# Half of the skip product moved one block earlier, input transposes put between its sums, and the norm's root moved to GpSimd, in the attention layer of a two-layer kernel

## The chip, the cores and the metric

The kernel runs on one core of a Trainium2 chip. The metric is the device time of one execution in microseconds (us); smaller is better. A core has five engines that each work through their own list of instructions in order: PE (TensorE, matrix products and transposes), ACT (ScalarE), DVE (VectorE), POOL (GpSimd) and SP (SyncE, which here issues nearly all DMA transfers). An instruction that needs another engine's result waits for a semaphore, and everything behind it on its own engine waits with it. That holds for SP too: a DMA whose source is not ready yet holds up the DMAs listed behind it.

## The reference

Two layers, each added to its input. The first one is an attention over 8 batches of 1024 tokens with 512 channels and 16 heads of 32; it is the one that the change touches. Cut to what matters:

```python
x = x * s1[:, None, :]                       # s1, s2: halves of cond
mu = jnp.mean(x, axis=-1, keepdims=True)
var = jnp.mean(jnp.square(x - mu), axis=-1, keepdims=True)
x = (x - mu) * jax.lax.rsqrt(var + EPS_IN)
q = heads(jnp.einsum('bsh,oh->bso', x, q_weight) * q_dc[:, None, :])
k = heads(jnp.einsum('bsh,oh->bso', x, k_weight) * k_dc[:, None, :])
v_flat = jnp.einsum('bsh,oh->bso', x, v_weight) * v_dc[:, None, :] * s2[:, None, :]
skip = v_flat
v = heads(v_flat)
attn = jax.nn.softmax(jnp.einsum('bhqd,bhkd->bhqk', q, k) * scale, axis=-1)
out = jnp.einsum('bhqk,bhkd->bhqd', attn, v).transpose(0, 2, 1, 3).reshape(B, S, H)
out = jnp.einsum('bsh,oh->bso', out, w_weight) * w_dc[:, None, :]
skip = jnp.einsum('bsh,oh->bso', skip, u_weight) * u_dc[:, None, :]
return out + skip
```

The second layer (a gated state-space scan over 1024 steps) follows and is not touched.

## The kernel before, in words

**Blocks and slots.** The attention is a hand-written pipeline. A batch b has four blocks o = 0 to 3; a block is four heads. A block has 16 slots: 8 query tiles of 128, times two pairs of heads. Slot n issues, in this order: in odd n only, the product of an earlier slot pair's probabilities with the values (`weigh`, L303, on PE); the scores of two heads (L286 and L289); their maxima on DVE (L447); transposes of the slot before's first head (`flip`, L296) with their copies on ACT (L454); the two exponentials on ACT (L457); some pieces of background work; the transposes of the second head, with their two copies on DVE (L468, L473); more pieces of background work; and the scaling of the probabilities by 1/sum on POOL (L462, L471, L476), which waits for reciprocals on DVE (L461, L470, L475). With `weigh` at the head of the odd slots, the time from one slot's first score product to the next slot's is longer behind an even slot than behind an odd one.

**Background pieces.** `background(n)` is a generator that yields once for each 128x512 product (four of them make one sum of a `chain`, L130) or for each group of four input transposes (`turn`, L111). Its work by block is: o = 0 and 1: the projections of the next block (`project`, 6 sums, 24 pieces), then half of the output product of the batch before (`out_w`, 4 sums, 16 pieces). o = 2: the projections of block 3 (24), then the transposes of the first half of the next batch's inputs (`turn`, 4). o = 3: the transposes of the second half (4), the projections of the next batch's first block (24), then the whole skip product (`out_u`, 8 sums, 32). Behind the projections, each block calls `fetch_w(n + 2)`, which loads the three weight tiles (w_q, w_k, w_v, 256 KB each, two buffers each) that the projections of the next block will use. What is left of a generator at the end of a block is run out before the next block starts.

**How many pieces a slot gets.** A table gives the pieces of a block, and `due` spreads them; `late` of them come behind the second transposes:

```python
PIECES = {0: 40, 1: 40, 2: 28, 3: 60}
few = max(1, (pieces - 2 * NQ + NQ) // SB)        # NQ = 8, SB = 16
due = few * (done - done // 2) + -(-(pieces - NQ * few) * (done // 2) // NQ) - ran
late = (due + 1 - n % 2) // 2
```

So with 28 pieces an even slot gets 1 and an odd one 2 or 3; with 40 it is 2 and 3; with 44 it would be 2 and 3 or 4; with 60 it is 3 and 4 or 5. The last block of all has its own line for `due`.

**Evacuations and buffers.** All sums and turns share one ring of two PSUM buffers (`ps_m`, tag "mm"), so a sum can start when the sum or turn two places before it has been copied out. The projections are copied out by ACT (L208, L212, L217), `out_u` and `out_w` by DVE with the addition of a loaded tile (L251, L267), and then stored by SP (`xu_d`, L252); turns are copied out by ACT for even k and by DVE for odd k (L113, L115). A finished q half is copied by SP to the other half of the partitions by two DMAs (`moved`, L201 and L202), which wait for ACT.

**The order on SP.** It is the order in which the generators reach their `dma_start`. In blocks 0, 1 and 2 the fetch of w_q, w_k, w_v stands behind the `moved` pair of the last q half of that block's projections; in block 3 too, with `out_u`'s loads (xr from xT, w_u) and stores behind it.

**The norm.** `aside(n)` loads the next batch's inputs in block 1 and runs `normalise` for one half in block 1 and for the other in block 2, one piece at the end of each slot: one slot with the loads, four multiplications on POOL (L84), four pairs of statistics on DVE (L88, L89), then in one piece the square root on ACT (L91), its reciprocal on DVE (L92) and one more small DVE operation (L93), and four scalings on POOL (L101). The piece with the root ends slot 9, so it stands just ahead of slot 10. The exponentials and the square root need different ACT tables, and each change between them is an ACT_TABLE_LOAD.

Of the kernel before, what the change touches and what calls it, by code (L numbers as in the profile page):

```python
# [8 lines left out]
F32 = mybir.dt.float32  # L9
BF16 = mybir.dt.bfloat16  # L10
AF = mybir.ActivationFunctionType
ALU = mybir.AluOpType
# [4 lines left out]
P = 128  # L17
B = 8
H = 512
KH = H // P  # L20
# [7 lines left out]
EPS = 1e-5  # L28
# [4 lines left out]
def modulated_attention(ctx, tc, const, xp, tok, x1_d, xu_d, S, x, xT, cond, wT, ident, condT, early, handover):  # L33
# [9 lines left out]
    nc = tc.nc  # L43
# [10 lines left out]
    own = ctx.enter_context(tc.tile_pool(name="own", bufs=1))  # L54
    sT = own.tile([P, 2 * KH, B], F32, name="sT")
    nc.sync.dma_start(out=sT, in_=condT.rearrange("(k p) b -> p k b", p=P))
    eps = own.tile([P, 1], F32, name="eps_h")
    nc.vector.memset(eps, EPS)
    dc = own.tile([P, 5, KH, B], F32, name="dc")
# [3 lines left out]
    def load_x(b, hf):  # L63

        xq = tok.tile([P, 4, H], F32, name="xq")
        src = x[b, hf * HW : (hf + 1) * HW].rearrange("(j p) c -> p j c", p=P)
        if b == 0:
            nc.sync.dma_start(out=xq[:, 0:2], in_=src[:, 0:2])
        else:
            nc.sync.dma_start(out=xq, in_=src)  # L70
        sr = tok.tile([P, H], F32, name="sr")
        nc.sync.dma_start(out=sr, in_=cond[b, 0:H].unsqueeze(0).to_broadcast([P, H]))
        if b == 0:
            nc.sync.dma_start(out=xq[:, 2:4], in_=src[:, 2:4])
        return xq, sr

    def normalise(xs, first=False):


        xq, sr = xs  # L80
        mv = small.tile([P, 4, 2], F32, name="mv")
        rs = small.tile([P, 4, 2], F32, name="rs")
        for j in range(4):
            (nc.vector if first else nc.gpsimd).tensor_mul(xq[:, j], xq[:, j], sr)  # L84
            yield
        for j in range(4):
            stat = small.tile([P, 6], F32, name="stat")
            nc.vector.bn_stats(stat, xq[:, j])  # L88
            nc.vector.bn_aggr(mv[:, j], stat)  # L89
            yield  # L90
        nc.scalar.activation(rs[:, :, 0], mv[:, :, 1], AF.Sqrt, bias=eps)  # L91
        nc.vector.reciprocal(rs[:, :, 0], rs[:, :, 0])  # L92
        nc.vector.scalar_tensor_tensor(  # L93
            rs[:, :, 1], mv[:, :, 0], -1.0, rs[:, :, 0], ALU.mult, ALU.mult
        )
        yield
        for j in range(4):
            if first and j % 2 == 0:
                nc.scalar.activation(xq[:, j], xq[:, j], AF.Identity, bias=rs[:, j, 1:2], scale=rs[:, j, 0:1])
            else:  # L100
                nc.gpsimd.tensor_scalar(xq[:, j], xq[:, j], rs[:, j, 0:1], rs[:, j, 1:2], ALU.mult, ALU.add)  # L101
            yield

    def turn(xs, put):

        xh = xp.tile([P, KH, HW], F32, name="xh")
        put(xh)
        for k in range(KH):
            ps = ps_m.tile([P, 4, P], F32, tag="mm", name="mm_ps")
            for j in range(4):  # L110
                nc.tensor.transpose(ps[:, j], xs[0][:, j, k * P : (k + 1) * P], ident)  # L111
            if k % 2 == 0:
                nc.scalar.copy(xh[:, k], ps.rearrange("p j t -> p (j t)"))  # L113
            else:
                nc.vector.tensor_copy(xh[:, k], ps.rearrange("p j t -> p (j t)"))  # L115
            yield
# [4 lines left out]
    def half(hf):  # L121
        return slice(hf * HW, (hf + 1) * HW)
# [3 lines left out]
    def chain(pieces, evac):  # L126

        ps = ps_m.tile([P, HW], F32, tag="mm", name="mm_ps")
        for k, (w, x) in enumerate(pieces):
            nc.tensor.matmul(ps, w, x, start=(k == 0), stop=(k == KH - 1))  # L130
            if k < KH - 1:
                yield
        evac(ps)
        yield
# [6 lines left out]
    def load_full(name, pool, tag):  # L141
        w = pool.tile([P, KH, H], F32, tag=tag, name="w")
        nc.sync.dma_start(out=w, in_=wT[name].rearrange("(k p) o -> p k o", p=P))
        return w
# [35 lines left out]
    def load_w(name, o, room=None):  # L180
        w = ring.tile([P, KH, P], F32, tag=f"w_{room or name}", name=f"w_{name}")
        nc.sync.dma_start(
            out=w, in_=wT[name][:, o * P : (o + 1) * P].rearrange("(k p) o -> p k o", p=P)
        )
        return w
# [47 lines left out]
    def load_xr(src, o, hf):  # L233
        xr = ring.tile([P, HW], F32, tag="xr", bufs=3, name="xr")
        nc.sync.dma_start(out=xr, in_=src[o * P : (o + 1) * P, half(hf)])
        return xr

    def out_u(b, vTs, w0):

        todo = [(o, hf) for o in range(KH) for hf in range(2)]  # L240
        ws, xrs = {0: w0}, {todo[0]: load_xr(xT[b], *todo[0])}
        for n, (o, hf) in enumerate(todo):
            c = half(hf)
            if n + 1 < len(todo):
                xrs[todo[n + 1]] = load_xr(xT[b], *todo[n + 1])
            if hf == 0 and o + 1 < KH:
                ws[o + 1] = load_w("u", o + 1)
            xr = xrs.pop((o, hf))

            def evac(ps):  # L250
                nc.vector.scalar_tensor_tensor(xr, ps, udc[:, o, b : b + 1], xr, ALU.mult, ALU.add)  # L251
                nc.sync.dma_start(out=xu_d[b % 2, o * P : (o + 1) * P, c], in_=xr)  # L252

            yield from chain([(ws[o][:, k], vTs[k][:, c]) for k in range(KH)], evac)
# [54 lines left out]
    sts = {bo: {} for bo in blocks}  # L309
# [3 lines left out]
    def fetch_w(n):  # L313

        if n < len(blocks):
            wts[n] = {name: load_w(name, blocks[n][1]) for name in "qkv"}
# [3 lines left out]
    first = [load_x(0, 0)]  # L320
# [16 lines left out]
        next(demods["v"])  # L337
    fetch_w(1)

    def background(n):  # L340

        nonlocal xh_now
        b, o = blocks[n]
        if o < 2 and b > 0:
            w0 = load_w("w", 2 * o)
        if o == KH - 1:
            w0 = load_w("u", 0)
        if n == 1:
            tables = early(xp.tile([P, KH * HW], F32, tag="xh", name="tmp"), ps_m)
            next(tables)  # L350
        if n == 0:
            yield from demods["v"]
            yield from project(
                wts[0], xh_now, 0, 0, sts[0, 0], (("v", 0), ("v", 1), ("q", 1))
            )
            rest = [load_full(name, tok, "xq") for name in "wu"]
        if o < KH - 1:
            yield from project(wts[n + 1], xh_now, b, o + 1, sts[b, o + 1])
            if o == 2 and b + 1 < B:
                yield from turn(xs_next[0], xh_next.append)  # L360
        elif b + 1 < B:
            yield from turn(xs_next[1], xh_next.append)
            xh_now = list(xh_next)
            xh_next.clear()
            yield from project(wts[n + 1], xh_now, b + 1, 0, sts[b + 1, 0])
        fetch_w(n + 2)
        if n == 0:
            yield from demod((3, 4), rest)
        if o < 2 and b > 0:
            yield from out_w(  # L370
                b - 1, [sts[b - 1, k]["a"] for k in range(KH)], [(k, hf) for k in (2 * o, 2 * o + 1) for hf in range(2)], {2 * o: w0}
            )
        if o == KH - 1:
            yield from out_u(b, [sts[b, k]["v"] for k in range(KH)], w0)
        if n == 1:
            yield from tables
        if n == len(blocks) - 1:
            ws = {k: load_w("w", k, "wqkv"[k]) for k in range(KH)}
            last_w.append(out_w(
                b, [sts[b, k]["a"] for k in range(KH)], [(o, hf) for hf in range(2) for o in range(KH)], ws  # L380
            ))
            yield
            for _ in range(4 * KH):
                yield next(last_w[0])
# [8 lines left out]
            yield from normalise(xs_next[o - 1])  # L393

    xs_next, xh_next, last_w = [], [], []
    PIECES = {0: 40, 1: 40, 2: 28, 3: 60}
    probs = None
    flipped = {}
    bg, side, ran, ripe = iter(()), iter(()), 0, 0
    for n in range(len(slots) + 2):  # L400
        bo, q, pair = slots[n] if n < len(slots) else (None, None, None)
        if n % SB == 0:
# [4 lines left out]
            bg, side, ran = iter(()), iter(()), 0  # L407
# [4 lines left out]
        due = 0  # L412
        if bo is not None:

            done, pieces = n % SB + 1, (54, 29)[n // SB] if n < 2 * SB else PIECES[bo[1]]
            few = max(1, (pieces - 2 * NQ + NQ) // SB)
            due = few * (done - done // 2) + -(-(pieces - NQ * few) * (done // 2) // NQ) - ran
            if n < 3:
                due = 6
            if n // SB == len(blocks) - 1:  # L420

                due = -(-33 * min(done, 10) // 10) + 16 * max(done - 10, 0) // 6 - ran
            due = max(due, 0)
            ran += due

# [2 lines left out]
        if n % 2 == 1 and m >= 0:  # L428
            mbo, mq, _ = slots[2 * m]
# [715 lines left out]
```

## Time and profile before

| what | value |
|---|---|
| median of 3 runs | 5712.75 us (5705.14 to 5713.35) |
| the profiled execution | 5708.03 us, its span 5706.3 us |
| busy share of the span | PE 97%, DVE 77%, ACT 69%, POOL 27% |
| first score product of the first slot | 52.3 us |
| first score product of the last slot | 3317.0 us |
| blocks 0, 1, 2, 3 of batch 2 | 98.01, 99.12, 92.99, 116.38 us |
| the last batch's blocks 0, 1, 2 | 98.01, 98.01, 91.57 us |
| mean granted TensorE clock | 0.991 |

The times of blocks and slots are differences between the starts of the first L286 of each, from the timeline of PE. The profiled execution stands 4.7 us under the median and 2.9 us over the fastest run. The attention takes some 3300 us of the span and the scan the rest. In the timeline a row is: start in us, duration in us, engine, line, operation, output <- inputs, form, count, and in brackets the idle time of the engine just before it with what ended it. An engine with a "q" behind its name is its instruction queue (SPq issues DMAs). One 128x512 product in f32 makes two matmul records, each about 0.43 us apart.

### The profile page before, as it was taken

The numbers are of one execution on the slowest core, as the hardware profiler recorded it, in microseconds if no ns is written. First come the engines' busy times: TensorE is split into PE (matmuls) and PEld (weight loads), VectorE is DVE, ScalarE is ACT, GpSimd is POOL, SyncE is SP. The second block draws the span as 40 slices with busy tenths as digits, with TensorE's granted clock in tenths as the row PEclk, the third lists the DMA queues.
The fourth block names the chain that finished last, engine by engine and source line by source line (L and its number), as shares of the span: only waits on it lengthen the run. The fifth ranks groups of instructions, "written<-read, shape, count | busy, mean of one in ns | idle before, by whom it ended". The sixth has DMA issues, their size and how long they took to land.

```text
span 5706.3 us, 113668 instructions
## 1 busy us (share of the span) xinstructions
PE 5525.4 (97%) x43312; PEld 3178.8 (56%) x43312; DVE 4382.9 (77%) x6874; ACT 3959.9 (69%) x6995; POOL 1540.4 (27%) x1667
## 2 busy tenths in 40 slices
PE   7999999999999999999999989999999999999998
PEld 4565656656556556656556555555555555555553
DVE  4666666766766766766666659999999999999996
ACT  5565655655655655655655558898988888888886
POOL 2343433433434434434433310111111111111111
PEclk9999999999999999999999989999999999999999
DMA  2102212112112112112021248888888888888886
GB/s 83 35 24 64 53 44 67 31 55 57 31 58 53 38 50 67 24 53 71 18 65 41 71 123 233 236 238 237 238 238 234 237 235 238 235 238 236 238 238 188
DMA packets 377216, 714.85 MB, mean 125 GB/s; under 512 B 198320, under 2 KB 280512, under 8 KB 347488
## 3 DMA queue, kind: packets, MB, share of 16 engines
q1 hardware_dynamic: 346704, 684.81, 44.4%
q0 software_dynamic: 29968, 22.77, 1.5%
q8 instruction: 344, 5.64, 0.4%
q14 instruction: 200, 1.64, 0.1%
HBM read 596.66 MB, written 83.89 MB: 119 GB/s over the span
## 4 chain that ended last, share of the span: by engine, by line
PE 63%; DMA 15%; DVE 9%; ACT 8%; issue 3%; SPq 2%; POOL 0%; DVEq 0%; ACTq 0%; POOLq 0%
PE mm_ps L130 17%; PE t_ps L296 15%; DMA xb<-xd 10%; PE s_ps L286 9%; PE t_ps L303 8%; DVE h L933 4%; PE in_ps L668 4%; PE y_ps L920 3%; ACT xb L911 2%; PE g_ps L823 2%; SPq L901 2%; DMA out<-o_sb 2%; ACT pr L457 2%; PE o_ps L860 1%; DMA xd<-xt 1%
## 5 line engine op out<-in xcount | busy, mean ns | idle before, releaser
L447 DVE TENSOR_REDUCE nmax<-s_ps 128x1 f32<-128x1024 f32 x1024 | 1206.2, 1220 | 460.7 <-PE s_ps L289 459.9
L454 ACT COPY pT<-t_ps 128x512 f32<-128x512 f32 x1024 | 550.3, 589 | 1298.9 <-PE t_ps L296 1298.4
L933 DVE CUSTOM_DVE_ANT_0 h<-h,xb,lim 128x1024 f32<-128x1024 f32 x1024 | 1373.5, 1341 | 90.0 <-ACT xb L911 41.2
L296 PEld LDWEIGHTS t_ps<-ident,pr 128*128 128x128 f32 x8192 | 912.2, 141 | 658.9 <-issue 491.7
L911 ACT ACTIVATE xb<-xb,ws 128x1024 f32<-128x1024 f32 x1024 | 1177.8, 1164 | 60.2 <-DMA xb<-xd 45.0
L457 ACT ACTIVATE pr<-s_ps,nmax 128x1024 f32<-128x1024 f32 x1024 | 1139.5, 1127 | 5.0 <-DVE nmax L447 4.8
L296 PE MATMUL t_ps<-ident,pr 128*128 128x128 f32 x8192 | 1096.9, 277 | 28.4 <-ACT pT L454 24.7
L476 POOL TENSOR_SCALAR pr<-pr,rinv 128x1024 f32<-128x1024 f32 x512 | 572.2, 1118 | 130.0 <-DVE rinv L475 123.0
L286 PE MATMUL s_ps<-kT,qT 32*128 32x512 f32 x2048 | 596.0, 641 | 2.5 <-ACT pr L457 1.7
L289 PE MATMUL s_ps<-k,q 32*128 32x512 f32 x2048 | 578.0, 640 | 1.1 <-DMA q<-qT 1.1
L462 POOL TENSOR_SCALAR pr<-pr,rinv 128x1024 f32<-128x1024 f32 x256 | 286.8, 1121 | 1070.7 <-PE t_ps L296 751.4
L920 PE MATMUL y_ps<-h,yw 128*32 128x512 f32 x4096 | 527.3, 610 | 36.6 <-DVE y_ps L755 31.6
L303 PEld LDWEIGHTS t_ps<-pT,vt 128*32 128x32 f32 x16384 | 433.9, 110 | 207.6 <-DVE rinv L470 112.9
L303 PE MATMUL t_ps<-pT,vt 128*32 128x128 f32 x16384 | 506.9, 274 | 19.1 <-DVE pT L468 12.3
L471 POOL TENSOR_SCALAR pr<-pr,rinv 128x1024 f32<-128x1024 f32 x256 | 286.2, 1118 | 844.6 <-DVE rinv L470 795.7
L668 PE MATMUL in_ps<-x,win 128*128 128x256 f32 x2048 | 492.2, 386 | 3.8 <-ACT xb L892 3.8
L823 PE MATMUL g_ps<-win,x1t 128*128 128x512 f32 x1024 | 470.5, 602 | 4.0 <-ACT x1t L818 3.6
L860 PE MATMUL o_ps<-wout,xt 128*128 128x512 f32 x1024 | 458.5, 595 | 0.0
L872 POOL DMA_DIRECT2D out<-o_sb x256 | 151.0, 595 | 1053.0 <-ACT o_sb L866 953.3
L668 PEld LDWEIGHTS in_ps<-x,win 128*128 128x128 f32 x2048 | 376.9, 193 | 95.2 <-ACT xb L892 26.2
L786 POOL DMA_DIRECT2D bca<-few x256 | 129.1, 515 | 1019.1 <-ACT few L779 1013.5
L468 DVE COPY pT<-t_ps 128x512 f32<-128x512 f32 x512 | 352.0, 687 | 56.1 <-PE t_ps L296 55.6
(157 smaller groups left out, 6975.4 us busy)
## 6 DMA issues: line engine op xcount, KB each, us to landing
xb<-xd SPq DMA_DIRECT2D x1792, 256.0 KB
xd<-xt SPq DMA_DIRECT2D x64, 512.0 KB
q<-qT SPq DMA_DIRECT2D x128, 128.0 KB
xr<-in_xT SPq DMA_DIRECT2D x64, 256.0 KB
xu_d<-xr SPq DMA_DIRECT2D x64, 256.0 KB
xr<-xu_d SPq DMA_DIRECT2D x64, 256.0 KB
x_d<-xr SPq DMA_DIRECT2D x64, 256.0 KB
out<-o_sb POOLq DMA_DIRECT2D x256, 64.0 KB, 6.0
```

What stands on the lines that cost most here:

```text
L130: nc.tensor.matmul(ps, w, x, start=(k == 0), stop=(k == KH - 1))
L286: nc.tensor.matmul(s_ps[i][:, 0:HW], st["q"][r, qc], st["k"][r, 0:HW], start=True, stop=True)
L289: nc.tensor.matmul(s_ps[i][:, HW:S], st["q2"][r, qc], st["k2"][r], start=True, stop=True)
L296: nc.tensor.transpose(ps[:, j], pr[:, c0 : c0 + P], ident)
L303: nc.tensor.matmul(av[r], vt[:, kt, r], pT[:, i, kt], start=(kt == 0), stop=(kt == KT - 1), skip_group_check=True,)
L447: nc.vector.tensor_reduce(nmax[i], s_ps[i], AX.X, ALU.max, negate=True)
L457: nc.scalar.activation(fresh[i], s_ps[i], AF.Exp, bias=nmax[i], accum_out=rsum[i])
L668: nc.tensor.matmul(ps, win[kk][:, k * P : (k + 1) * P], st["x1"][:, kk].rearrange("p b t -> p (b t)"), start=(kk == 0), stop=False,)
L823: nc.tensor.matmul(ps, st["xo", i][:, k], win[k][:, DI + half * 512 : DI + (half + 1) * 512], start=(k == 0), stop=(k == KH - 1),)
L911: nc.scalar.mul(xbs[n], xbs[n], sts[c]["ws"][:, t : t + 1])
L920: nc.tensor.matmul(st["y", i][32 * r : 32 * r + 32, hf * 512 : (hf + 1) * 512], yws[i][:, 4 * q + r, :], hs[4 * g + r][:, hf * 512 : (hf + ...
L933: nc.vector._custom_dve(dve_ops.TENSOR_ADD_SAT, out=h, in0=last["h"], in1=xbs.pop(n), s0=lim[:, 0, t : t + 1], s1=lim[:, 1, t : t + 1],)
```

## The change

Three things change in the attention. `out_u` gets a list of output tiles `os` and is called twice: for tiles 0 and 1 in block 2, and for tiles 2 and 3 in block 3, each time with its first w_u tile loaded at the block's start. `between` puts one turn behind each of its four sums. In block 3, the projections of the next batch's first block now come behind that, last in the block. `PIECES` becomes 44 and 44 in place of 28 and 60 (16 + 4 + 24 pieces in both), and the last block's rate falls from 33 to 17 pieces in its first ten slots. In `normalise`, for all but the two halves of the first batch, the root and its reciprocal become an addition of EPS and a power of -0.5 on POOL, both on 128x4; L93 on DVE takes their result.

```diff
+    halves = own.tile([P, 4], F32, name="halves_h")
+    nc.vector.memset(halves, -0.5)
...
-        nc.scalar.activation(rs[:, :, 0], mv[:, :, 1], AF.Sqrt, bias=eps)
-        nc.vector.reciprocal(rs[:, :, 0], rs[:, :, 0])
+        if first:
+            nc.scalar.activation(rs[:, :, 0], mv[:, :, 1], AF.Sqrt, bias=eps)
+            nc.vector.reciprocal(rs[:, :, 0], rs[:, :, 0])
+        else:
+            nc.gpsimd.tensor_scalar(rs[:, :, 0], mv[:, :, 1], EPS, None, ALU.add)
+            nc.gpsimd.tensor_tensor(rs[:, :, 0], rs[:, :, 0], halves, ALU.pow)
...
-    def out_u(b, vTs, w0):
-
-        todo = [(o, hf) for o in range(KH) for hf in range(2)]
-        ws, xrs = {0: w0}, {todo[0]: load_xr(xT[b], *todo[0])}
+    def out_u(b, vTs, os, w0):
+
+        todo = [(o, hf) for o in os for hf in range(2)]
+        ws, xrs = {os[0]: w0}, {todo[0]: load_xr(xT[b], *todo[0])}
...
-            if hf == 0 and o + 1 < KH:
+            if hf == 0 and o + 1 in os:
                 ws[o + 1] = load_w("u", o + 1)
...
+    def between(chains, others):
+
+        for n, _ in enumerate(chains):
+            yield
+            if n % KH == KH - 1:
+                for _ in others:
+                    yield
+                    break
+
     def background(n):
...
-        if o == KH - 1:
-            w0 = load_w("u", 0)
+        if o >= 2:
+            w0 = load_w("u", 2 * (o - 2))
...
         if o < KH - 1:
             yield from project(wts[n + 1], xh_now, b, o + 1, sts[b, o + 1])
-            if o == 2 and b + 1 < B:
-                yield from turn(xs_next[0], xh_next.append)
-        elif b + 1 < B:
-            yield from turn(xs_next[1], xh_next.append)
+        if o >= 2:
+            yield from between(
+                out_u(b, [sts[b, k]["v"] for k in range(KH)], (2 * (o - 2), 2 * (o - 2) + 1), w0),
+                turn(xs_next[o - 2], xh_next.append) if b + 1 < B else iter(()),
+            )
+        if o == KH - 1 and b + 1 < B:
             xh_now = list(xh_next)
             xh_next.clear()
             yield from project(wts[n + 1], xh_now, b + 1, 0, sts[b + 1, 0])
         fetch_w(n + 2)
...
-        if o == KH - 1:
-            yield from out_u(b, [sts[b, k]["v"] for k in range(KH)], w0)
...
-    PIECES = {0: 40, 1: 40, 2: 28, 3: 60}
+    PIECES = {0: 40, 1: 40, 2: 44, 3: 44}
...
-                due = -(-33 * min(done, 10) // 10) + 16 * max(done - 10, 0) // 6 - ran
+                due = -(-17 * min(done, 10) // 10) + 16 * max(done - 10, 0) // 6 - ran
```

## The prediction

> **What bounds the kernel now.** I read the page's shares first (PE 97%), then the busy time of each engine by block, then the PE timeline of one batch, whose time from one slot's first score product (L286) to the next I list by the pieces it holds. Batches 1 to 6 agree within 0.03 us in each block, so batch 2 stands for all. Its four blocks:
>
> ```profile
> 888.14:986.15 98.01, 97.91 (x985) 59.84 (x984) 66.24 (x107) 57.02 (x104) 35.04 (x32) 1.00 0.18 44
> 986.15:1085.27 99.12, 98.38 (x985) 59.96 (x984) 69.72 (x119) 59.98 (x107) 43.53 (x40) 1.00 0.26 70
> 1085.27:1178.26 92.99, 89.02 (x969) 56.30 (x968) 66.67 (x115) 59.42 (x107) 42.41 (x39) 1.00 0.10 24
> 1178.26:1294.64 116.38, 114.81 (x1033) 68.18 (x1032) 72.00 (x118) 59.71 (x109) 37.27 (x34) 1.00 0.18 55
> ```
>
> The columns are: length, then busy us of PE, weight load, DVE, ACT and POOL, granted clock, DMA share, GB/s. PE is full in blocks 0, 1 and 3, and idle 4 us in block 2, the one with few pieces. Slots by pieces: even ones last 6.23 us with 1 piece, 6.57 with 2, 7.43 with 3; odd ones 4.05 with none, 4.69 with 2, 5.55 with 3, 6.41 with 4, 7.26 with 5; a group of value transposes (L230) adds 0.43. A piece costs PE 0.86 where PE bounds; below 2 pieces an even slot is bounded by the chain maxima - copy L468 - copy L473 - `weigh`, and a piece saved there gives 0.34 only. That is the room the change can use: pieces go from slots at 0.86 to slots at 0.34. Block 3 also waits in its first slot, where turns follow each other and the ring has two buffers:
>
> ```profile
> 1182.85 0.60 PE L111 MATMUL mm_ps<-ident,xq 128*128 128x128 f32 x4
> 1185.02 0.65 PE L111 MATMUL mm_ps<-ident,xq 128*128 128x128 f32 x4 [1.57 <-ACT xh L113]
> ```
>
> That slot takes 9.22 us in place of 7.43.
>
> **Moving the sums and turns.** A turn takes PE 0.46 us (next start 0.44 to 0.46 later), 0.40 less than a piece. Block 2 after, with 44 pieces: slots 0 to 8 hold the 24 projection pieces: 5 x 6.57 + 2 x 6.41 + 2 x 5.55 + 0.86 for two value transposes = 57.63. Slots 9 to 15 hold four sums and four turns: 6.41; 7.50 (the norm's slot, below); 5.55; 6.85 (a turn's DVE copy of 0.68 comes ahead of L468, so `weigh` starts later: 3.57 + 0.68 + 2 x 0.7 + 1.0 us and the small steps between); 6.01; 6.57; 5.15. Sum 101.67, against 92.99. Block 3 after: eight even slots of 6.57, and the odd ones 6.00, 5.95, 6.80, 5.15, 6.84, 5.55, 6.41, 5.98. In the second and third of these, the sum behind an early turn waits some 0.75 us for the buffer of the sum ahead of that turn, whose DVE copy ends 4.9 us into the slot (so it does for L267 in batch 2). Sum 101.24, against 116.38: -15.14. Both blocks together: -6.46 a batch.
>
> **The root on POOL.** The slot that now holds the table loads is 7.68 us in block 1 (6.57 in batch 7, which has none), 7.67 in block 2. Its rows:
>
> ```profile
> 1047.77 1.28 ACT L91 ACT_TABLE_LOAD   x1
> 1047.96 1.12 POOL L476 TENSOR_SCALAR pr<-pr,rinv 128x1024 f32<-128x1024 f32 x1 [0.40 <-DVE rinv L475]
> 1049.61 0.16 DVE L93 SCALAR_TENSOR_TENSOR rs<-mv,rs 128x4 f32<-128x4 f32 x1
> 1049.69 2.35 DVE L447 TENSOR_REDUCE nmax<-s_ps 128x1 f32<-128x1024 f32 x2
> ```
>
> The maxima (L447) are queued on DVE behind L93, and without the root would start at 1048.85. After the change L93 waits for POOL, whose two small operations stand behind the scaling L476, which ends at 1049.08. So the wait only changes its owner: DVE now waits for POOL. The trace shows neither small operation. From below: POOL's 128x1 memsets take 0.10. From above: a 128x512 tensor product (L84) takes 1.27, a 128x512 scaling (L101) 0.76; with 1.12 for 128x1024 that leaves 0.40 for a scaling of nearly nothing. I take 0.8 for both together, nearest the last number; ends 0.2 and 2.5, the upper one for a power that costs more than any product. Then L93 ends near 1050.2 and the maxima start 0.5 later than now, but the second table load of 1.28 ahead of the exponential falls away, and `weigh` waits for L468 and L473 as before: 7.5 us for 7.68, -0.18 in block 1 (already in block 2's sum). If the cover gives out (POOL 1 us slower), the slot is 1 us longer, 14 times.
>
> The Trainium skill, "ScalarE: Activation LUTs", section "What ACT_TABLE_LOAD costs", prices a switch at 2.66 us with the engine's drain, two of them here; by that, an estimate, the change would save 5.3 us a root, 74 us in all, but the trace has 1.11 and 1.44 us on the slots. The skill's "GPSIMD Engine Reference", section "Instruction dispatch", speaks against the change: the first call of freshly loaded code costs about 6 us; by that, an estimate, the power would add 6 us once, and no run here shows it.
>
> So far: a batch of 406.50 becomes 98.01 + 98.94 + 101.67 + 101.24 = 399.86, -6.64.
>
> **What becomes late: two weight loads a batch.** SP issues in order. Today the fetch for the next block stands behind the last q half's `moved` pair, and in no block is that less than some pieces before its use. In block 3 after, the projections end with the block: the last q piece ends slot 15, ACT copies it (0.70) until 0.5 us into the next slot, the pair takes 0.46 + 0.60, and w_q, w_k, w_v are issued from 1.7 us on. w_v is the first weight that block 0's slot 0 uses, 2.0 us in, and everything on PE stands behind it. Likewise w_u for tiles 2 and 3 is the fourth load behind the last xu_d store of block 2, whose DVE copy ends about 0.3 us before block 3 starts; it is issued with the three others from 0.2 us on, and block 3's first piece needs it at 2.0 (as 1196.33 stands 2.0 behind the L286 at 1194.33). What four such loads cost when nothing is ahead, the end of the last block shows (SPq, then PE):
>
> ```profile
> 3283.42 2.14 SPq L182 DMA_DIRECT2D w_w<-in_wwT  x4
> ```
>
> ```profile
> 3286.80 1.12 PE L130 MATMUL mm_ps<-aT,w_w 128*128 128x512 f32 x2 [1.37 <-DMA w_w<-in_wwT]
> ```
>
> The first load releases PE 3.38 us after its issue. The following ones come 0.82 us apart (256 KB at the 321 GB/s of that window). So w_v, third, is there at 1.7 + 3.38 + 1.64 = 6.7: PE waits 4.7, say 4.8 with the semaphore. w_u, fourth, at 0.2 + 3.38 + 2.46 = 6.0, plus up to 0.8 for the store ahead: PE waits 4.3. And PE does not come back at full speed. The last block's first slot, where w_u stands behind the four w_in loads, shows it by the granted clock (the column of 1.00 and 0.50):
>
> ```profile
> 3210.86:3214.27 3.41, 0.77 (x8) 0.53 (x5) 2.10 (x2) 3.04 (x5) 0.12 (x1) 1.00 1.01 362
> 3214.27:3217.68 3.41, 2.49 (x3) 1.17 (x4) 0.00 (x0) 0.23 (x2) 0.00 (x0) 0.50 0.30 87
> 3217.68:3221.10 3.42, 3.42 (x11) 2.27 (x10) 1.15 (x3) 0.00 (x0) 0.31 (x1) 0.50 0.00 0
> 3221.10:3224.51 3.41, 3.41 (x72) 2.10 (x70) 1.12 (x3) 0.00 (x0) 1.90 (x2) 1.00 0.07 25
> ```
>
> After 3.56 us idle, PE worked from 3215.19 to 3221.10 at half clock: 2.95 us lost. The slot took 16.20 us; at 4 pieces it would be 8.29. After 3.15 us idle (at 273) the clock stayed at 1.00. Idle times of 4.3 to 4.8 are above both; where they fall against these steps of 3.41 us decides between some 1.5 and 3; I take 2.4. So 7.2 and 6.7 us for the two waits. Each comes 7 times (w_v in batches 1 to 7, w_u in batches 0 to 6): 7 x 13.9 = 97.3.
>
> **First and last batch.** Batch 0: block 1 -0.2, block 2 +8.7, block 3 -15.1: -6.6. Batch 7 has no turns: block 2 with 40 pieces is 57.63 + 41.79 = 99.42, +7.85. The last block's slots 1 to 9 fall from 58.33 to 48.26, -10.07; its first slot's w_u comes later by some 2.6 us (the w_in loads now stand behind the last xu_d store) with two pieces fewer, +0.6: -1.6 in all. The rest, scan included, has no changed instruction: 0.
>
> **Sum.** -6.6 - 6 x 6.64 - 1.6 = -48.0 gained, 97.3 lost: +49. On the profiled execution's 5708 that is 5757; the median of the runs stands 4.7 above it. I give 5759.
>
> **The rivals.**
> - *The loads are in time* (**faster**). For it: PE has idle time in block 2, 1.57 us of a ring wait goes, weights are double buffered. Against: the order on SP. It decides from a price of 48.0 / 14 = 3.4 us a wait downwards. 5660. If only one of the two is hidden, 5707 to 5711.
> - *The waits come, the clock holds*: 7 x (4.8 + 4.3) = 63.7, +16: 5724. For it: the 3.15 us gap without a drop. Against: the 3.56 us one with it.
> - *The power is slow*: 2.5 us for the pair adds 1.7 to 14 slots, +24: 5782.
>
> **How the numbers follow.** Forecast 0.58; loads in time 0.12; one hidden 0.07; clock holds 0.15; slow power 0.08. The range of 5705 to 5795 takes in all but the first rival: below, waits of 3.4 us; above, 8.5 us a wait (the last block's row plus the store) with a slow power. About 0.2% of the time, 11 us, is what can be told from no change here: the first rival and the low tail of the others are faster (0.14), the half-hidden case and a little of the clock case within it (0.08), the rest slower (0.78).
>
> **What would show it.** Block times of batch 2: 105, 99, 102, 108 us. PE waits <- DMA w_v and <- DMA w_u of more than 3 us, seven each, followed by stretches at clock 0.50. No 1.57 us wait at L113, no L91 table load after the first batch. DVE waits for POOL ahead of L93, 14 times. It is wrong if w_v is issued on SP before the last q copy, or if slot 0 of blocks 0 and 3 stay at 6.6 us.

## The result, and the profile after

The changed kernel takes 5760.79 us (median of 5 runs, 5748.41 to 5764.12) against 5710.32 for the kernel before (5 runs, 5705.14 to 5713.35): a ratio of 1.0086 [1.0071, 1.0101], slower by 50.5 us. The prediction said 5759.

The profiled execution took 5764.12 us, span 5762.3, mean granted clock 0.983 for 0.991. From the first slot to the last, the attention takes 3312.7 us where it took 3264.7: +48.0. What follows the attention takes 8.7 us more in this execution, with the same instructions in the same order; that part differs from one profiled execution to the next (2389.3 us in the kernel before, 2385.9 to 2400.5 in the eight kernels of the experiments), and the medians stand only 50.5 apart. So it is the attention's +48.0 that has to be explained.

The four blocks of batch 2 after, by the busy times of the engines (columns as in the prediction: length, PE, weight load, DVE, ACT, POOL, clock, DMA share, GB/s):

```profile
894.27:999.72 105.45, 100.46 (x985) 61.13 (x984) 65.65 (x106) 57.85 (x106) 35.48 (x32) 0.97 0.20 49
999.72:1099.06 99.34, 97.99 (x985) 59.84 (x984) 69.45 (x118) 57.16 (x104) 44.82 (x42) 1.00 0.26 70
1099.06:1200.06 101.00, 99.89 (x1001) 61.81 (x1000) 70.00 (x119) 58.33 (x106) 44.45 (x42) 1.00 0.13 35
1200.06:1307.63 107.57, 102.10 (x1001) 62.77 (x1000) 69.12 (x114) 57.37 (x105) 36.09 (x34) 0.98 0.13 40
```

Read the first row against the 98.01 of before. Block 0 holds the same instructions of PE as before (x985), yet is 7.44 us longer: PE is idle for 4.99 us (105.45 - 100.46; 0.10 before), and the clock of 0.97 is the rest, for PE's own busy time has grown by 2.55. Block 3 is 8.8 us shorter than it was, but again idle for 5.5 us and at 0.98. Blocks 1 and 2 run at 1.00 and are full.

The view of waits, PE's own (what was waited for: us in total, times, the longest), names the two:

```profile
PE mm_ps L136 <- DMA w_u<-in_wuT: 35.5, 8, 5.2
...
PE mm_ps L136 <- DMA w_v<-in_wvT: 32.7, 7, 5.1
```

The eighth w_u is that of the last block, which waited before the change too. How the w_v wait comes about is seen at the start of batch 3 (1307.63), on SP's queue and then on PE:

```profile
1308.02 0.46 SPq L207 DMA_DIRECT2D q<-qT  x1
1308.52 0.60 SPq L208 DMA_DIRECT2D q<-qT  x1
1309.16 0.59 SPq L188 DMA_DIRECT2D w_q<-in_wqT  x1
1309.79 0.56 SPq L188 DMA_DIRECT2D w_k<-in_wkT  x1
1310.39 0.51 SPq L188 DMA_DIRECT2D w_v<-in_wvT  x1
```

```profile
1314.85 2.07 PE L136 MATMUL mm_ps<-xh,w_v 128*128 128x512 f32 x2 [5.05 <-DMA w_v<-in_wvT]
```

The pair of q copies has to wait for ACT's copy of the last q sum, which now belongs to the last slot of block 3; the three loads have no input to wait for, but stand behind the pair. w_v lands 4.5 us after its issue, 7.2 us into the block, and PE stood still from 1309.80. Two matmuls that take 1.02 us at full clock (experiment 1 shows them) then take 2.07: the clock is down. The busy times in steps of 3.41 us around it, with the clock in the third column from the right:

```profile
1308.76:1312.17 3.41, 1.04 (x11) 0.80 (x8) 2.35 (x2) 2.77 (x5) 0.00 (x0) 1.00 0.77 203
1312.17:1315.58 3.41, 0.73 (x1) 0.50 (x2) 0.00 (x0) 0.50 (x2) 0.00 (x0) 0.50 0.63 184
1315.58:1318.99 3.41, 3.41 (x11) 2.27 (x10) 1.08 (x3) 0.00 (x0) 0.25 (x1) 0.50 0.00 0
1318.99:1322.40 3.41, 3.41 (x74) 2.00 (x72) 0.73 (x3) 0.00 (x0) 1.96 (x2) 1.00 0.02 5
```

Behind a step in which PE was busy for 1.04 us, and again behind one with 0.73, the next step is granted at 0.50; behind a full step it is back at 1.00. Work done at 0.50 costs half its time: (0.73 + 3.41) / 2 = 2.07 us. With the 5.05 of idling that is 7.1 of the 7.35 us by which this block exceeds 98.01.

The w_u wait comes about in the same way. Block 3 of batch 2 starts at 1200.06; its w_u is issued fourth, behind the last store of block 2 and the three loads of the fetch, and PE stands still until it has landed (SP's queue, then PE):

```profile
1199.86 0.33 SPq L258 DMA_DIRECT2D xu_d<-xr  x1
1200.24 0.42 SPq L188 DMA_DIRECT2D w_q<-in_wqT  x1
1200.72 0.55 SPq L188 DMA_DIRECT2D w_k<-in_wkT  x1
1201.31 0.51 SPq L188 DMA_DIRECT2D w_v<-in_wvT  x1
1201.92 0.45 SPq L188 DMA_DIRECT2D w_u<-in_wuT  x1
```

```profile
1206.14 1.90 PE L136 MATMUL mm_ps<-vT,w_u 128*128 128x512 f32 x2 [3.90 <-DMA w_u<-in_wuT]
```

Seven waits for w_v and seven for w_u (without the last block's) leave PE idle for 64.1 us. The fourteen blocks exceed their undisturbed length (98.01 for block 0, 101.34 for block 3 as experiment 3 has it) by 50.7 + 48.3 = 99.1 us. The other 35.0 is what follows the waits, the slow clock above all (experiment 4); what else is in it was not separated.

### The profile page after: what moved, and what is told of

The parts are those of the page before. It is cut to its first block, busy times and chain, and to the rows that moved or that the text cites. A ratio compares the mean times of both kernels' runs of the same rounds, so it can differ in the third digit from the quotient of the medians.

```text
span 5762.3 us, 113680 instructions
## 1 busy us (share of the span) xinstructions
PE 5537.3 (96%) x43312; PEld 3189.9 (55%) x43312; DVE 4379.4 (76%) x6861; ACT 3922.2 (68%) x6953; POOL 1558.3 (27%) x1695
## 4 chain that ended last, share of the span: by engine, by line
PE 65%; DMA 16%; DVE 9%; ACT 4%; SPq 3%; issue 2%; POOL 1%; DVEq 0%; ACTq 0%; POOLq 0%
PE mm_ps L136 18%; PE t_ps L302 15%; DMA xb<-xd 12%; PE s_ps L292 9%; PE t_ps L309 8%; PE in_ps L683 4%; DVE h L948 4%; PE y_ps L935 3%; SPq L916 2%; PE g_ps L838 2%; ACT xb L926 2%; PE o_ps L875 1%; DMA xd<-xt 1%; DVE nmax L462 1%; DMA out<-o_sb 1%
## 5 line engine op out<-in xcount | busy, mean ns | idle before, releaser
L302 PEld LDWEIGHTS t_ps<-ident,pr 128*128 128x128 f32 x8192 | 926.9, 142 | 658.2 <-issue 508.0
```

The source lines that it names most:

```text
L302: nc.tensor.transpose(ps[:, j], pr[:, c0 : c0 + P], ident)
```

## The experiments

Two theories stood against each other. **The order on SP**: the change is worth some 48 us, and two loads a batch that come late through SP's order take that back twice. **The work itself**: the new order of pieces, the turns between the sums or the root on POOL cost the time, and the waits for loads only show where PE would have waited anyway. Further experiments size the parts: the clock, the root, the place of the turns. Experiments 1 to 4 ran on one chip (the kernel before 5709.97 us there, 19 runs), 5 to 8 on another (5708.94, 15 runs).

**1. The fetch ahead of block 3's projections.** It undoes the w_v wait alone.

```diff
             xh_next.clear()
+            fetch_w(n + 2)
             yield from project(wts[n + 1], xh_now, b + 1, 0, sts[b + 1, 0])
-        fetch_w(n + 2)
+        else:
+            fetch_w(n + 2)
```

> Edit: in block 3 the fetch of w_q, w_k, w_v stands ahead of the last projections, not behind them; all else as in the changed kernel. Theory (the fetch is late because it stands behind the last q half's copies on SP): block 0's first slot goes from 13.9-14.0 us to 6.57, seven times, -7.4 x 7 = -52 against the changed kernel: about 5709 us, that is the same as the kernel before within 5 us. No PE wait for DMA w_v is left; the waits for w_u stay. Rival 1 (the first slot of block 0 is long for another reason, such as the copies of the last sums of block 3): 5761, the slot stays near 14. Rival 2 (the wait only moves on to the next weight or to the q halves' copies): at most half of it goes, 5735 or more.

Measured: 5710.75 us, 0.9999 [0.999, 1.0008] of before, so 50 us below the changed kernel. The loads are issued some 55 us before the block that uses them (first fence, SP's queue), the q pair comes at 1294.53 as late as ever, and the first product with w_v, 2.0 us into block 0, waits for nothing (second fence, PE):

```profile
1237.69 1.22 SPq L188 DMA_DIRECT2D w_q<-in_wqT  x1
1238.97 0.50 SPq L188 DMA_DIRECT2D w_k<-in_wkT  x1
1239.51 0.51 SPq L188 DMA_DIRECT2D w_v<-in_wvT  x1
```

```profile
1296.15 1.02 PE L136 MATMUL mm_ps<-xh,w_v 128*128 128x512 f32 x2
```

Block 0 is 98.01 us in every batch from 1 on. The waits for w_u stay: 36.9 us, eight times. One of the two waits is worth what was said, and the other doesn't take its place.

**2. The third w_u tile loaded in block 2.** It undoes the w_u wait alone.

```diff
+            if n == len(todo) - 1 and os[0] == 0:
+                ahead.append(load_w("u", 2))
...
-            w0 = load_w("u", 2 * (o - 2))
+            w0 = load_w("u", 0) if o == 2 else ahead.pop()
```

> Edit: the w_u tile for the first sum of block 3 is loaded ahead of the last of the four sums of block 2, so on SP it stands ahead of that sum's store and of the fetch; all else as in the changed kernel. Theory: block 3's first slot goes from 12.4-14.6 us to 6.57 in batches 0 to 6 (-6.5 on average, -45), and in batch 7, where it now also stands ahead of the w_in loads, from 14.6 to about 6.6 (-8): -53 against the changed kernel, about 5708 us. The waits for w_v stay. Rival 1 (the slot is long because a turn's copy on DVE stands ahead of the maxima, not because of the load): 5761 less the 8 of batch 7 at most. Rival 2 (the 256 KB only displace another load): the next tile's load (w_u for the second pair of sums) becomes the wait, at most half is won, 5735.

Measured: 5705.94 us, 0.9992 [0.9983, 1.0002]. Block 3 is 101.3 to 101.7 us in batches 0 to 6, the last block's first slot 7.66 us where it took 14.63; the w_v waits stay (34.7 us, seven times).

**3. Both.**

> Edit: both of the above, the fetch ahead of block 3's projections and the w_u tile ahead of block 2's last sum. Theory (two separate waits, each with the slow clock behind it, are all that the change loses): the two gains add, -105 against the changed kernel: 5656 us, 0.95% faster than the kernel before. Blocks of batch 2: 98.0, 99.3, 101.0, 101.2 us; granted clock 1.00 in all of the attention behind batch 0. Rival (the even spreading itself gains nothing and the 48 us were an artefact of my adding up slots): 5711, the same as before.

Measured: 5660.86 us, 0.9914 [0.99, 0.9929]: 100 us below the changed kernel and 49 below the one before. The blocks of batch 2, to be held against those of the changed kernel:

```profile
878.08:976.09 98.01, 97.91 (x985) 59.83 (x984) 65.49 (x106) 57.86 (x106) 35.48 (x32) 1.00 0.18 44
976.09:1075.42 99.33, 97.98 (x985) 59.84 (x984) 69.44 (x118) 57.15 (x104) 44.81 (x42) 1.00 0.26 70
1075.42:1176.42 101.00, 99.89 (x1001) 61.80 (x1000) 70.00 (x119) 58.33 (x106) 44.43 (x42) 1.00 0.14 38
1176.42:1278.12 101.70, 100.16 (x1002) 61.67 (x1001) 68.98 (x114) 57.38 (x105) 36.08 (x34) 1.00 0.15 48
```

The middle two are as in the changed kernel to 0.01 us; the outer two have lost 7.4 and 5.9 us, and both their clocks are 1.00. (The last row's 101.70 is 101.33 to 101.34 in the other batches; a whole batch is 399.69.) No work was taken out, and the loads are the same in number and size. That settles the first question: the whole loss was the time at which two loads were issued, and the theory of the work itself falls.

**4. Five unread products ahead of the first piece.** The changed kernel with its late loads; ahead of the first piece of blocks 0 (from batch 1) and 3, PE multiplies an already present k by the identity, and nobody reads the sum. The waits stay, PE is busy in them.

```diff
             w0 = load_w("u", 2 * (o - 2))
+        if o == KH - 1 or (o == 0 and b > 0):
+            ps = ps_m.tile([P, HW], F32, tag="mm", name="mm_ps")
+            for _ in range(5):
+                nc.tensor.matmul(ps, ident, sts[b, o]["k"][:, 0:HW], start=True, stop=True)
```

> Edit: the changed kernel with five 128x512 products whose result nobody reads (4.3 us of PE work) ahead of the first piece of blocks 0 (batches 1 to 7) and 3, that is, in the place where PE waits for the weights. Theory (the wait costs its 4 to 5 us and then half a clock for the work behind it): the waits shrink to under 1 us, the first slots still end as late as the load allows, but at clock 1.00: 12.0 in place of 14.0 in block 0, 10.6 in place of 12.4 in block 3, -2.0 x 14 = -28: about 5733 us, and the stretches at 0.50 in the attention are gone. Rival 1 (what is lost behind the wait is a backlog on ACT and DVE, not the clock): unchanged slots, 5761. Rival 2 (the added products come on top): 5761 + 14 x 4 = 5817.

Measured: 5733.16 us, 1.0038 [1.0023, 1.0053], so 27.6 us less than the changed kernel for 75 products more (15 places: the edit reaches the last block too, which takes 98.98 us for 98.58). PE at the start of batch 3's block 0, and then the steps of 3.41 us:

```profile
1301.47 4.46 PE L366 MATMUL mm_ps<-kT,ident 128*128 128x512 f32 x10
1306.73 1.12 PE L136 MATMUL mm_ps<-xh,w_v 128*128 128x512 f32 x2 [0.80 <-DMA w_v<-in_wvT]
```

```profile
1303.41:1306.82 3.41, 2.61 (x7) 0.85 (x5) 0.00 (x0) 1.10 (x3) 0.00 (x0) 1.00 0.85 233
1306.82:1310.23 3.41, 3.41 (x40) 2.12 (x44) 1.42 (x4) 0.00 (x0) 0.97 (x1) 1.00 0.03 8
```

The first product with w_v still comes 7.3 us into the block, but it runs at full clock (1.12 in place of 2.07 us), and no stretch of 0.50 is left between 272 and 3303 us. In batch 2, block 0's first slot is 11.75 us for 14.00, block 3's 10.93 for 12.43. So of the 7.1 us that a wait cost on average, some 27.6 / 14 = 2.0 was the clock (the fourteen blocks themselves are 29.2 us shorter). It may be a little more, since in three places no wait for w_u is left, so that the added products may have held the work up there.

**5. The root on POOL, alone, in the kernel before.**

> Edit: the kernel before, with nothing changed but the root on GpSimd. Theory (the wait on DVE only changes its owner: 0.24 + 1.04 us on POOL, behind a scaling, for two table loads on ACT): the slot behind the root goes from 7.68 to about 7.9 us in both blocks, +0.2 x 14 = +3: 5713, not to be told from before. Rival 1 (the table loads were the price of the slot): the slot falls to 6.6 in block 1 and 6.2 in block 2, -2.5 a batch: 5692. Rival 2 (each pair of table changes costs the 5.3 us of the notes): 5636.

Measured: 5710.66 us, 1.0005 [0.9996, 1.0014]: no difference that can be told. Blocks 1 and 2 are each 0.2 us longer (99.33 and 93.21), their slots with the root 7.89 us: by the blocks that part of the change costs 0.4 us a batch, some 3 us in all, as expected. Neither rival came: leaving out the table loads saves nothing here as long as DVE waits for the root all the same.

**6. The corrected kernel of experiment 3 with the root back on ACT.**

> Edit: the version with both loads early (5661 us), with the root back on ACT as in the kernel before. Theory: the root's place is worth nothing here either; slot 10 of block 1 7.68 in place of 7.90, that of block 2 (7.04, where a turn stands in the place of a product) between 7.0 and 7.7: 5661 within 5 us. Rival (the root on GpSimd is a part of what the early loads could show): 5675 or more.

Measured: 5658.02 us, 0.9911 [0.9896, 0.9926]; blocks of 98.01, 99.12, 101.15 and 101.35. The same as experiment 3 within the runs' spread: with the loads in time too, it doesn't matter which engine takes the root as long as DVE waits for it.

**7. The corrected kernel with the turns behind the four sums, not between.**

```diff
-            yield from between(
-                out_u(b, [sts[b, k]["v"] for k in range(KH)], (2 * (o - 2), 2 * (o - 2) + 1), w0),
-                turn(xs_next[o - 2], xh_next.append) if b + 1 < B else iter(()),
-            )
+            yield from out_u(b, [sts[b, k]["v"] for k in range(KH)], (2 * (o - 2), 2 * (o - 2) + 1), w0)
+            if b + 1 < B:
+                yield from turn(xs_next[o - 2], xh_next.append)
```

> Edit: the version with both loads early (5661 us), with the four turns of a block in a row behind the four sums, not one behind each sum. Theory (what the change gains is the even number of pieces; the turns' places between the sums bring a wait for the sum's copy, 0.35 to 0.85 us in two slots of block 3, which now goes, against a ring wait between the turns): the same within 8 us, 5653 to 5669. Rival (turns in a row wait for the ring as in block 3 of the kernel before, about 2.7 us a block): 5661 + 14 x 2.7 = 5699.

Measured: 5656.61 us, 0.9904 [0.989, 0.9917]. Block 2 is 0.8 us longer (101.79), block 3 0.6 shorter (100.72), the batch 399.86 for 399.69. So putting the turns between the sums brings nothing that can be told. In a row they wait for the ring once a batch (6.5 us in seven waits, the longest 0.9, where it was 1.57 in the kernel before); between the sums, the sums wait for the copies of sums twice a batch (8.7 us in fourteen). One is worth about the other.

**8. The corrected kernel, DVE's part of the root one slot later.** What DVE waits for in the changed kernel is seen on POOL and then on DVE, in batch 2's block 1:

```profile
1061.54 1.12 POOL L491 TENSOR_SCALAR pr<-pr,rinv 128x1024 f32<-128x1024 f32 x1 [0.40 <-DVE rinv L490]
1062.74 0.24 POOL L97 TENSOR_SCALAR rs<-mv 128x4 f32<-128x4 f32 x1
1063.06 1.04 POOL L98 TENSOR_TENSOR rs<-rs,halves_h 128x4 f32<-128x4 f32 x1
```

```profile
1064.13 0.16 DVE L99 SCALAR_TENSOR_TENSOR rs<-mv,rs 128x4 f32<-128x4 f32 x1 [2.76 <-POOL rs L98]
```

The maxima of the next slot are queued behind this operation, which needs 0.16 us and waits for 2.76. A `yield` between the pair on POOL and L99 puts it one slot on:

```diff
             nc.gpsimd.tensor_tensor(rs[:, :, 0], rs[:, :, 0], halves, ALU.pow)
+            yield
```

> Edit: the version with both loads early (5661 us), with the small DVE operation that takes the root's result moved one slot behind the two POOL operations. Theory (the root costs because DVE stands and waits for POOL with the maxima behind it): DVE's 14 waits of 1 to 2.8 us for POOL go, slot 10 falls from 7.90 to 6.57 in block 1 and from 7.04 to about 6.6 in block 2: -1.8 x 7 = -12: 5649. Rival (POOL's 1.28 us delay the scalings and so the transposes of the next slot): the slot keeps 7.0 or more, 5656 to 5661.

Measured: 5642.26 us, 0.988 [0.9866, 0.9893], the fastest of all. The blocks of batch 2:

```profile
868.70:966.71 98.01, 97.91 (x986) 59.82 (x985) 65.48 (x106) 57.91 (x106) 35.60 (x32) 1.00 0.19 44
966.71:1064.72 98.01, 97.91 (x986) 59.82 (x985) 69.71 (x118) 57.08 (x104) 44.92 (x42) 1.00 0.27 71
1064.72:1164.92 100.20, 99.82 (x1002) 61.79 (x1001) 70.16 (x119) 58.25 (x106) 44.57 (x42) 1.00 0.14 38
1164.92:1266.62 101.70, 100.16 (x1002) 61.67 (x1001) 68.96 (x114) 57.43 (x105) 36.20 (x34) 1.00 0.16 48
```

Block 1 loses 1.33 us against experiment 3 and is as long as block 0, which has no norm in it; block 2 loses 0.80; DVE has no wait for POOL left. Over the attention of the two profiled executions it is 18.7 us (3192.6 for 3211.3), of which six whole batches give 12.7, about the 12 expected for all, and batch 0 gives 6.0. As the edit gives 2.1 in a whole batch, the rest of the 6.0 is batch 0's own spread: its first block, the same in every kernel here, took 110.3 to 113.7 us. So what the root cost in experiment 3 was not POOL's time but DVE's wait for it. Whether the root on ACT could be had as cheaply in this way was not tried.

## Why the prediction was right

The time, the sign and the cause came out as put down: two weight loads a batch late through the order on SP, each followed by half clock. The signs came too: the blocks of batch 2 were put at 105, 99, 102 and 108 us and took 105.45, 99.34, 101.00 and 107.57; DVE waits for POOL 14 times, and no table load of the root is left behind the first batch. The last step of the sum is loose: 5757 and 4.7 make 5762, not 5759; with the later median of 5710.32 its +49 gives 5760. By its steps:

- **Pieces and slots.** Forecast without the waits: 98.01 + 98.94 + 101.67 + 101.24 = 399.86. Experiment 3, which is the change without the waits, has 98.01 + 99.33 + 101.00 + 101.34 = 399.69. Two terms are off, in opposite directions: block 1 by 0.4, block 2 by 0.7. Most of the second is block 2's slot with the norm, put at 7.5, which was 7.04: DVE copies out a sum there and then waits for POOL 1.21 us, where it waits 2.76 in block 1. That the two nearly cancel is luck.
- **Idle time for the two loads.** Forecast 7 x (4.8 + 4.3) = 63.7; measured 64.1 (single waits of 4.35 to 5.05 us for w_v, 3.89 to 5.18 for w_u). The row of the last block, with four loads and nothing ahead of them, was a good measure for these: a w_v was put at 4.8 and was 4.7 on average, a w_u at 4.3 and was 4.5.
- **Half clock.** Forecast 2.4 a wait, 33.6; measured 35.0 by difference, of which experiment 4 shows some 27.6 to be the clock. The 2.4 was a choice between 1.5 and 3, not worked out, so that it came this near is in part luck. The prediction left open where a wait falls against the steps of 3.41 us, and that is indeed what spreads it. A w_u wait of 3.90 us in batch 2 falls on one step and costs one step at 0.50; block 3 took 6.2 us too long. One of 4.93 us in batch 4 falls so that a step with 2.46 us of work goes at 0.50 as well, and the block took 8.1 too long. The busy times by steps, of the changed kernel, the shorter case first:

```profile
1202.95:1206.36 3.41, 0.22 (x1) 0.22 (x2) 1.00 (x1) 2.30 (x4) 0.00 (x0) 1.00 1.06 326
1206.36:1209.77 3.41, 3.41 (x11) 2.27 (x11) 0.76 (x2) 0.00 (x0) 0.00 (x0) 0.50 0.31 92
...
2032.38:2035.79 3.41, 2.46 (x5) 1.32 (x6) 0.00 (x0) 0.00 (x0) 0.00 (x0) 0.50 0.54 182
2035.79:2039.20 3.41, 3.41 (x21) 1.87 (x23) 1.52 (x4) 0.00 (x0) 1.98 (x2) 0.50 0.00 0
```

  The Trainium skill, "TensorE: Matmul & The Clock Gate", section "What's actually happening", has a free-running window of 3413 ns after which the clock is set anew; the steps here agree. It asks for an idle window before the clock drops; here a step with 1.04 us of work in 3.41 was enough, and the measurement decides.
- **The root on POOL.** Mis-sized: the pair takes 1.28 us, not 0.8, the power alone 1.04. With that the slot grew by 0.2 us in block 1 (7.90 for 7.68) where -0.18 was forecast: 0.4 us in each block 1, some 3 us in all. The 6 us for a first call don't show: the first power took 1.05 us (at 227.25), right behind the addition. The point that DVE's wait only changes its owner held, and experiment 8 shows what the prediction did not draw from it: the wait could be had away for nothing.
- **First and last batch.** Batch 0 got 0.7 us shorter where, with its w_u wait (6.7 - 6.6), +0.1 was forecast; with its own spread of some 3 us that tells nothing. The last block fell by 10.2 us (forecast 9.5), but not as worked out. Its w_u was expected 2.6 us later and came 0.55 later (7.46 us into the block for 6.91), so its first slot took 14.63 us (forecast 16.8; 2.6 less two pieces of 0.86 would be +0.9, not +0.6). Slots 1 to 9 took 50.73 (forecast 48.26), and the same in experiment 3, so the late load is not what makes them longer; what does stays open. Here too, two errors nearly cancel.
- **The rivals.** The loads in time was put at 5660; experiment 3 makes that case and takes 5660.86. One of the two hidden was put at 5707 to 5711; experiments 1 and 2 take 5710.75 and 5705.94. The clock that holds was put at 5724; experiment 4, the nearest to it, takes 5733 with its extra work and waits. The slow power did not happen.

## What to carry to other kernels

When a step is moved, follow its loads as well as its products: on a queue that issues in order, a load with no input of its own is as late as the copy ahead of it, and moving work to the end of a stage can put the next stage's weights behind that stage's last result. Issue such loads ahead of the step whose result blocks the queue; here a few moved lines turn +50 us into -49. Price a wait of the bounding engine as its length plus the slow clock behind it, and when a small operation moves to another engine, look at who waits for it there before asking how fast that engine is.

## What the runs showed of the hardware

- A power on POOL over 128x4 f32 took 1.04 us (14 times, no first one longer: 1.05 us at 227.25), nearly as much as a scaling of 128x1024 (1.12). An addition on the same tile took 0.24.
- Behind the fourteen waits the clock dropped after steps of 3.41 us with 0.00 to 1.06 us of PE work; in experiment 4 it held after the step shown with 2.61. PE's busy time alone doesn't decide: after a step with 1.48 us it held in the kernel before (271.98) and dropped in experiment 1 (779.66), and in batch 0 of experiment 2 it dropped after one with 2.61 (264.90). Where a wait falls against the steps matters as well, and with it how much of its price is clock: a wait of 4.73 us (w_u in batch 1) brought one step at 0.50, one of 4.50 us (w_v in batch 1) two.
- Products that nobody reads, put into a wait, can be worth it where the wait can't be removed: 75 of them gave back 27.6 us.
